# Mean squares moved to ScalarE, and the values of two batches made beside the first GLU, in a two-layer gated cross-attention kernel

## Chip, cores and metric

The kernel runs on one core of a Trainium2 chip. The metric is the device time of one execution in microseconds (us), as the median of several runs. Before the change it is 2046.36 us, the median of three runs from 2041.12 to 2047.37. Five engines work side by side: TensorE (PE, matrix products), VectorE (DVE), ScalarE (ACT), GpSimd (POOL) and SyncE (SP), which here issues the DMA transfers. PEld is the weight load of PE.

## The reference, cut to what matters

The input x has 4 batches of 512 rows with 512 columns. Four gated residual parts follow one another: a state space scan, a GLU with quantised weights (the "bitnet"), a cross-attention with 16 heads of 128, and four small experts. The attention is the part that the change touches:

```
q = (hidden_states @ Wq).reshape(B, Sq, H, D)
k = (encoder_hidden_states @ Wk).reshape(B, Skv, H, D)
v = (encoder_hidden_states @ Wv).reshape(B, Skv, H, D)
q = rmsnorm(q, gq)
k = rmsnorm(k, gk)
scores = jnp.einsum('bqhd,bkhd->bhqk', q, k) * scale
attn = jax.nn.softmax(scores, axis=-1)
out = jnp.einsum('bhqk,bkhd->bqhd', attn, v)
```

Here rmsnorm is x * rsqrt(mean(x * x) + eps) * g. The values v depend on the context and on Wv alone, not on x, so they can be made at any time once both are there.

## The kernel before

**Numbers in halves.** Almost every 32-bit matrix operand is held as two 16-bit pieces, a high part hi and a remainder lo, and one product is three matmuls (mm3, L241). The helper split (L236) makes the two pieces: ScalarE writes hi (L238), then VectorE computes w * S - hi into lo (L239). Nearly all matmuls share L247, so the text tells them apart by the name of the result: pw is a piece of the values, pk of the keys, pq of the queries, ps of the scores, pav of the weighted sum.

**The stages.** A prologue runs the scan of batch 0 and then its GLU (bitnet(0), L1190). Beside it the kernel makes the values of batch 0 (first_values, L1198), stages the weights of the first four heads (L1200) and makes their keys (L1201). The prologue's tiles lie in the pool pro (L1142). When that pool is given back, a pool named at (L1204) takes the room, and it holds nearly all the tiles of the attention. The main loop (L1228) then walks over 4 x 16 heads. Under the attention of batches 0, 1 and 2 it lays the scan and the GLU of the next batch; under that of batch 3 it lays the experts of the first three batches. The experts of the last batch end the program.

**Values.** For a group of four heads hg, values_of (L348) makes four pieces of 128 rows, each by six matmuls into one PSUM bank and a split. For batches below PRE (here 1) first_values (L358) does this in the prologue. It loads Wv, takes its norm (L365), splits it (L366) and stores it to DRAM; then each piece is written to a tile ov, of which there are VB = 2, and stored to DRAM (L374). In the attention, values(hg) (L830) loads these pieces back with four DMAs (L838) into tiles named v, of which there are AV = 4. For the other batches values(hg) loads the split Wv (L842) and calls values_of in the attention itself, with the same tiles.

**Keys and query norms.** keys (L779) makes one piece of 128 rows by six matmuls. ScalarE sums the squares of each of four heads (L802). A VectorE instruction turns the sums into mean + eps, ssk (L805); GpSimd takes the power -1/2, rk (L178, called at L807); VectorE multiplies (L813); ScalarE and GpSimd split the result (L820, L822); two transposing DMAs store it as kT (L824). query_norms (L862) sums the squares of the queries on PE (psq, L868), VectorE adds eps and scales, ssq (L873), GpSimd takes the power, rqs (L178, called at L875), and ScalarE uses rqs in nmx (L896) and in the exponential pr (L904).

**What sets the order.** Every engine works its own queue in order. The queues are laid out at build time: the program's order is the rank, and a simulated timeline (L1342) fills an engine's free time with later work that is ready in it. So the pieces of the values, which come in the program after the GLU, can run inside it. All DMAs go through the one queue of SP, and a DMA at its head that waits holds up those behind it.

Of the kernel before, what the change touches and what calls it, by code (L numbers as in the profile page):

```python
# [29 lines left out]
F32 = mybir.dt.float32  # L30
# [4 lines left out]
AF = mybir.ActivationFunctionType  # L35
ALU = mybir.AluOpType
# [4 lines left out]
P = 128  # L41
B = 4
L = 512
T = 4
# [7 lines left out]
HD = 128  # L52
# [7 lines left out]
QS = 2.0**-11  # L60
KS = 1024.0
# [38 lines left out]
VB = 2  # L100
# [2 lines left out]
ABUF = {"m": 2, "s": 2}  # L103
LO_POOL = {(b, h, 1) for b in range(3) for h in range(9, 16)}
HL = 2
PRE = 1
LEADS = {1: 12, 2: 16, 3: 16}
LEAD_B = 6

# [2 lines left out]
def flamingo_kernel(  # L112
# [8 lines left out]
    nc = tc.nc  # L121
# [114 lines left out]
    def split(w, hi, lo, S):  # L236

        nc.scalar.activation(hi, w, AF.Copy, scale=S)  # L238
        nc.vector.scalar_tensor_tensor(lo, w, S, hi, ALU.mult, ALU.subtract)  # L239

    def mm3(ps, pairs, first=True, last=True):  # L241

        n = 3 * len(pairs)
        i = 0
        for lh, ll, rh, rl in pairs:
            for l, r in ((lh, rh), (lh, rl), (ll, rh)):
                nc.tensor.matmul(ps, l, r, start=first and i == 0, stop=last and i == n - 1)  # L247
                i += 1
# [3 lines left out]
    Sq, Sk, Sv, So, ceq = [], [], [], [], []  # L252
# [9 lines left out]
    def run(steps):  # L262
        while True:
            try:
                next(steps)
            except StopIteration as e:
                return e.value
# [60 lines left out]
    def attention_weights(hg, ps_pool, staging):  # L328
        cols = slice(hg * 512, (hg + 1) * 512)
        d, S, _ = yield from staging(f"wq{hg}", Wq[hg], HG, ps_pool)  # L330
        wq_d.append(d)
        Sq.append(S)
        d, S, _ = yield from staging(f"wk{hg}", Wk[:, cols].rearrange("(k p) c -> p k c", p=P), 1, ps_pool)
        wk_d.append(d)
        Sk.append(S)
        d, S, _ = yield from staging(f"wo{hg}", Wo[cols, :].rearrange("(h p) f -> p h f", p=P), HG, ps_pool)
        wo_d.append(d)
        So.append(S)

        c = const.tile([P, 1], F32, name=f"ceq{hg}")  # L340
        nc.vector.tensor_scalar(c, Sq[hg][:, 1:2], XS * QS * (HD * EPS) ** 0.5, None, ALU.mult)
        nc.vector.tensor_tensor(c, c, c, ALU.mult)
        ceq.append(c)

    wv_d = []
    v_d = [[dram.tile([P, T, 1024], F16, name=f"vd{b}{hg}") for hg in range(NG)] for b in range(PRE)]

    def values_of(b, hg, wv, ps_tile, v_tile):  # L348

        for c in range(T):  # L350
            rows = slice(c * P, (c + 1) * P)
            ps = ps_tile(f"pw{b}{hg}{c}")
            mm3(ps, [(cT[b][:, 0, k, rows], cT[b][:, 1, k, rows], wv[:, 0, k], wv[:, 1, k]) for k in range(2)])
            v = v_tile([P, 2, 512], F16, f"v{b}{hg}{c}")
            split(ps, v[:, 0], v[:, 1], QS)
            yield v

    def first_values(pool, ps_tile):  # L358


        for hg in range(NG):
            raw = pool.tile([P, 2, 512], F32, tag="rv", name=f"rawv{hg}", bufs=2)
            nc.sync.dma_start(raw, Wv[:, hg * 512 : (hg + 1) * 512].rearrange("(k p) c -> p k c", p=P))
            wv = pool.tile([P, 2, 2, 512], F16, tag="wv", name=f"wv{hg}", bufs=2)
            S = frobenius(raw, wv[:, 0], psv, f"wv{hg}")  # L365
            split(raw, wv[:, 0], wv[:, 1], S[:, 1:2])  # L366
            Sv.append(S)
            wv_d.append(dram.tile([P, 2048], F16, name=f"dwv{hg}"))
            nc.sync.dma_start(wv_d[hg], wv.rearrange("p s k c -> p (s k c)"))
            for b in range(PRE):  # L370
                for c, v in enumerate(
                    values_of(b, hg, wv, ps_tile, lambda s, d, n: pool.tile(s, d, tag="v", name=f"o{n}", bufs=VB))
                ):
                    nc.sync.dma_start(v_d[b][hg][:, c, :], v.rearrange("p s c -> p (s c)"))  # L374
                    yield
# [109 lines left out]
    gfac = const.tile([P, 1], F32, name="gfac")  # L485
# [276 lines left out]
    def attention(b):  # L762
# [16 lines left out]
        def keys(hg, ps_tile=ap):  # L779

            nm = f"{b}{hg}"
            wk = ak.tile([P, 2, 2, 512], F16, tag="wk", name=f"wk{nm}", bufs=1)
            nc.sync.dma_start(wk.rearrange("p s k c -> p (s k c)"), wk_d[hg])

            sck = sm(1, "sck", f"sck{nm}")
            nc.vector.tensor_scalar(
                sck, Sc[b][:, 1:2], Sk[hg][:, 1:2], EPS**0.5 / KS, ALU.mult, ALU.mult
            )
            nc.vector.tensor_tensor(sck, sck, sck, ALU.mult)
            kTs = []  # L790
            for pair in range(2):
                kTs.append(ak.tile([P, T, 2, 2, P], F16, tag="kT", name=f"kT{nm}{pair}", bufs=KT))
            kns[hg] = kTs
            for c in range(T):
                rows = slice(c * P, (c + 1) * P)
                ps = ps_tile(f"pk{nm}{c}")
                mm3(ps, [(c_[:, 0, k, rows], c_[:, 1, k, rows], wk[:, 0, k], wk[:, 1, k]) for k in range(2)])
                sq = ak.tile([P, L], F32, tag="sq", name=f"ksq{nm}{c}", bufs=2)
                ssk = sm(HG, "ssk", f"ssk{nm}{c}")
                for h in range(HG):  # L800
                    cols = slice(h * HD, (h + 1) * HD)
                    nc.scalar.activation(  # L802
                        sq[:, cols], ps[:, cols], AF.Square, accum_out=ssk[:, h : h + 1]
                    )
                nc.vector.tensor_scalar(ssk, ssk, 1.0 / (HD * KS * KS), sck, ALU.mult, ALU.add)  # L805
                rk = sm(HG, "rk", f"rk{nm}{c}")
                rsqrt(rk, ssk)  # L807
                if b in KACT:
                    for h in range(HG):
                        cols = slice(h * HD, (h + 1) * HD)  # L810
                        nc.scalar.activation(sq[:, cols], ps[:, cols], AF.Copy, scale=rk[:, h : h + 1])
                else:
                    nc.vector.tensor_tensor(  # L813
                        sq.rearrange("p (h d) -> p h d", h=HG), ps.rearrange("p (h d) -> p h d", h=HG),
                        rk.unsqueeze(2).to_broadcast([P, HG, HD]), ALU.mult,
                    )

                ks = ak.tile([P, 2, 2, 2 * HD], F16, tag="ks", name=f"ks{nm}{c}", bufs=2)
                kn = sq.rearrange("p (a d) -> p a d", a=2)
                (nc.vector.tensor_copy if KSD else nc.scalar.copy)(ks[:, :, 0], kn)  # L820
                eng = nc.vector if (b, hg) in KLD else nc.gpsimd
                eng.tensor_tensor(ks[:, :, 1], kn, ks[:, :, 0], ALU.subtract)  # L822
                for pair in range(2):
                    nc.sync.dma_start_transpose(  # L824
                        kTs[pair][:, c].rearrange("p s h r -> p (s h) r"),
                        ks[:, pair].rearrange("p s d -> p (s d)"),
                    )
                yield

        def values(hg):  # L830
            def v_tile(shape, dtype, name):
                return at.tile(shape, dtype, tag="v", name=name, bufs=AV)

            if b < PRE:
                vals[hg] = []
# [26 lines left out]
        def query_norms(i):  # L862
            hg, h = divmod(i, HG)
            hn = f"{b}{hg}{h}"
            sq = kqs[i][2]
            ps = ap(f"psq{hn}")
            for c in range(T):
                nc.tensor.matmul(  # L868
                    ps[:, c : c + 1], sq[:, c * P : (c + 1) * P], ones[:, 0:1],
                    start=True, stop=True,  # L870
                )
            ssq = sm(T, "ssq", f"ssq{hn}")
            nc.vector.tensor_scalar(ssq, ps[:, 0:T], ceq[hg], gfac, ALU.add, ALU.mult)  # L873
            rqs = sm(T, "rqs", f"rqs{hn}")
            rsqrt(rqs, ssq)  # L875
            kqs[i][2] = rqs
# [88 lines left out]
        def step(i, phase):  # L965
# [4 lines left out]
            if phase == 0:  # L970
                if h == 0:
# [3 lines left out]
                    if KL == 0 and kns[hg] is None:  # L975
                        run(keys(hg))
                    if b < PRE:
                        values(hg)
# [163 lines left out]
    with tc.tile_pool(name="pro", bufs=1) as pro, tc.tile_pool(name="psp", bufs=4, space=PSUM) as psp:  # L1142
# [52 lines left out]
        def aside(name):  # L1195
            return psum(pss, name)

        run(first_values(pro, aside))  # L1198
        for hg in range(EARLY):
            stage_attention_weights(hg, pss)  # L1200
        run(keys(0, aside))  # L1201
    psa = ctx.enter_context(tc.tile_pool(name="psa", bufs=4, space=PSUM))
    at_pool = ctx.enter_context(ExitStack())
    at = at_pool.enter_context(tc.tile_pool(name="at", bufs=1))  # L1204
# [22 lines left out]
    n = B * NH  # L1227
    for i in range(-2, n):  # L1228
# [13 lines left out]
        s = steps[(i + 1) // NH]((i + 1) % NH, 1) if 0 <= i + 1 < n else iter(())  # L1242
        w = steps[i // NH](i % NH, 2) if i >= 0 else iter(())
        for k, g in enumerate((q, s, q, s, w, s, w, s, w, q)):
# [7 lines left out]
            if k in KPOS:  # L1252
                j, c = divmod((i + 2) * len(KPOS) + KPOS.index(k) - KOFF, 4 * len(KPOS))
# [92 lines left out]
```

## Time and profile before

| what | value |
|---|---|
| median of three runs | 2046.36 us |
| the profiled execution | 2033.87 us |
| its span, first to last instruction | 2032.1 us |
| mean granted clock of PE | 0.882 |
| busy: PE, DVE, ACT, POOL | 1588.9, 1596.6, 1269.7, 1003.6 us |
| share of the span: PE, DVE, ACT, POOL | 78%, 79%, 62%, 49% |
| DMA queue of SP: bytes, share of 16 engines' span | 356.36 MB, 69.1% |

No engine is the limit from end to end, so the shares are read by stretch. The view of busy time by stretch gives, for each piece of the span, how long each engine worked in it; an engine that works nearly all of a piece is what that piece waits for. The groups of instructions by name give counts, durations and waits. The timeline lists instructions in order, with the idle time before each and what ended it.

### The profile page before, as it was taken

How to read it: one execution, taken by the hardware profiler on the slowest of the kernel's cores; microseconds unless marked ns; L12 is line 12 of the kernel's file. 1: busy time of each engine (PE TensorE's matmuls, PEld its weight loads, DVE VectorE, ACT ScalarE, POOL GpSimd, SP SyncE). 2: the span in 40 equal slices, each digit the busy share in tenths (PEclk: the TensorE clock that was granted, in tenths of full speed). 3: DMA queues.
4: the chain of work that ended last, by engine and by line, in shares of the span. 5: the costliest groups of instructions: out<-in, count | busy, mean ns of one | idle time of the engine just before them, and what ended most of it. 6: DMA issues, size and time to landing. Idle time of an engine off the chain costs nothing. (4 is left out here: it accounts for less than half of the span.)

```text
span 2032.1 us, 26952 instructions
## 1 busy us (share of the span) xinstructions
PE 1588.9 (78%) x8238; PEld 896.8 (44%) x8238; DVE 1596.6 (79%) x2975; ACT 1269.7 (62%) x2962; POOL 1003.6 (49%) x920
## 2 busy tenths in 40 slices
PE   4465855886768968788698977788989879798888
PEld 2343322444444424455444434455444445445446
DVE  6798984789999866999898669999985565655654
ACT  6786565766557565665447674656565676757653
POOL 1984341367676454867545367775354440413211
PEclk8555977888789979898799988899999999998999
DMA  7454468678889764777867568688675877857754
GB/s 258 155 194 157 126 172 248 154 204 179 209 239 221 169 126 133 182 180 185 204 144 160 113 156 222 163 194 225 164 158 125 175 171 198 193 171 171 193 123 136
DMA packets 525201, 358.07 MB, mean 176 GB/s; under 512 B 424768, under 2 KB 427456, under 8 KB 519040
## 3 DMA queue, kind: packets, MB, share of 16 engines
q1 hardware_dynamic: 525056, 356.36, 69.1%
q8 instruction: 64, 1.05, 0.2%
q14 instruction: 81, 0.66, 0.1%
HBM read 214.98 MB, written 38.54 MB: 125 GB/s over the span
## 5 line engine op out<-in xcount | busy, mean ns | idle before, releaser
L181 POOL TENSOR_TENSOR h<-du,bc 128x512 f32<-128x512 f32 x256 | 332.8, 1320 | 74.5 <-PE py L578 57.6
L578 PE MATMUL py<-ident,h 128*128 128x128 f32 x1024 | 194.1, 337 | 91.3 <-DVE h L603 74.3
L595 ACT ACTIVATE dA<-delta,A 128x512 f32<-128x512 f32 x256 | 171.7, 684 | 144.7 <-DVE h L603 113.1
L247 PE MATMUL ps<-kT,qT 128*128 128x512 f16 x768 | 212.8, 397 | 54.4 <-ACT pr L904 43.0
L602 DVE TENSOR_TENSOR_SCAN dA<-dA,h 128x512 f32<-128x512 f32 x200 | 240.6, 1218 | 10.3 <-ACT dA L595 7.0
L247 PE MATMUL pq<-axnT,wq 128*128 128x512 f16 x768 | 213.7, 437 | 41.4 <-DMA axnT<-xsa 15.5
L247 PE MATMUL pav<-pT,v 128*128 128x256 f16 x1536 | 200.2, 283 | 42.5 <-DVE v L239 14.5
L578 PEld LDWEIGHTS py<-ident,h 128*128 128x128 f32 x1024 | 164.7, 214 | 130.8 <-DVE h L603 100.6
L925 DVE SCALAR_TENSOR_TENSOR hl<-pr,den,hl 128x512 f16<-128x512 f32 x214 | 194.6, 924 | 26.5 <-ACT hl L922 15.0
L904 ACT ACTIVATE pr<-ps,nmx,rqs 128x512 f32<-128x512 f32 x256 | 197.7, 775 | 24.3 <-DVE hl L925 20.3
L884 DVE TENSOR_REDUCE nmx<-ps 128x1 f32<-128x512 f32 x256 | 172.8, 681 | 46.9 <-PE ps L247 46.3
L247 PEld LDWEIGHTS <-v 128*128 128x128 f16 x1536 | 154.2, 102 | 96.1 <-issue 33.7
L247 PE MATMUL pwo<-wo,oT 128*128 128x512 f16 x768 | 183.0, 389 | 11.6 <-DVE oT L239 4.5
L247 PEld LDWEIGHTS <-wq 128*128 128x128 f16 x768 | 84.3, 111 | 160.3 <-issue 96.8
L924 POOL TENSOR_SCALAR hl<-pr,den 128x512 f16<-128x512 f32 x86 | 63.3, 736 | 183.9 <-DVE den L911 107.3
L247 PEld LDWEIGHTS <-cT 128*128 128x128 f16 x768 | 79.7, 104 | 148.2 <-issue 78.2
L247 PEld LDWEIGHTS <-qT 128*128 128x128 f16 x768 | 77.7, 102 | 139.8 <-issue 76.1
L896 ACT ACTIVATE nmx<-nmx,rqs 128x1 f32<-128x1 f32 x256 | 69.3, 293 | 107.6 <-POOL rqs L178 64.7
L603 DVE TENSOR_TENSOR h<-dA,cc 128x512 f32<-128x512 f32 x200 | 134.0, 679 | 2.7
L181 POOL TENSOR_TENSOR g<-g,gv 128x512 f32<-128x512 f32 x64 | 84.2, 1318 | 95.2 <-DVE gv L707 44.8
L247 PE MATMUL pk<-wk,cT 128*128 128x512 f16 x384 | 107.9, 424 | 27.2 <-DVE ssq L873 15.9
L178 POOL TENSOR_TENSOR rqs<-ssq,mhalf 128x4 f32<-128x4 f32 x64 | 68.6, 1072 | 121.6 <-DVE ssq L873 112.0
(381 smaller groups left out, 3505.7 us busy)
## 6 DMA issues: line engine op xcount, KB each, us to landing
bc<-bd SPq DMA_DIRECT2D x112, 256.0 KB, 4.2
cc<-bd SPq DMA_DIRECT2D x112, 256.0 KB, 4.3
wq<-dwq SPq DMA_DIRECT2D x64, 256.0 KB, 3.9
wo<-dwo SPq DMA_DIRECT2D x64, 256.0 KB, 4.2
w<-w3d SPq DMA_DIRECT2D x12, 1024.0 KB, 7.1
g<-in_gate_b SPq DMA_DIRECT2D x48, 256.0 KB, 3.9
gv<-in_val_b SPq DMA_DIRECT2D x48, 256.0 KB, 4.1
de<-hle SPq DMA_DIRECT2D x9, 1024.0 KB, 4.8
```

What stands on the lines that cost most here:

```text
L178: nc.gpsimd.tensor_tensor(res, arg, mhalf[:, : arg.shape[1]], ALU.pow)
L181: nc.gpsimd.tensor_tensor(out, a, b, ALU.mult)
L247: nc.tensor.matmul(ps, l, r, start=first and i == 0, stop=last and i == n - 1)
L578: nc.tensor.matmul(ys[g // gs][:, g % gs, t, :], src[:, g::T], ident, is_transpose=True, start=first and t == 0 and g % gs == 0, stop=last ...
L595: last = nc.scalar.activation(dA, delta[:, t0 + t, :], AF.Exp, scale=A[:, t0 + t, n : n + 1])
L602: nc.vector.tensor_tensor_scan(dA, dA, h, 0.0, ALU.mult, ALU.add)
L603: nc.vector.tensor_tensor(h, dA, cc, ALU.mult)
L884: nc.vector.tensor_reduce(nmx[:, c : c + 1], ps, AX.X, ALU.max, negate=True)
L896: nc.scalar.activation(nmx[:, one], nmx[:, one], AF.Copy, scale=rqs[:, one])
L904: mark[0] = nc.scalar.activation(pr, scs[c], AF.Exp, bias=nmx[:, one], scale=rqs[:, one], accum_out=den[:, c - c0 : c - c0 + 1],).ins
L924: nc.gpsimd.tensor_scalar(hl[:, c, 0], prs[c], den[:, one], 1.0, ALU.mult, ALU.mult)
L925: nc.vector.scalar_tensor_tensor(hl[:, c, 1], prs[c], den[:, one], hl[:, c, 0], ALU.mult, ALU.subtract)
```

## The change

It has three parts.

1. The two small instructions ssk and ssq go from VectorE to ScalarE. ScalarE computes scale * in + bias, so ssq's form (p + c) * g becomes p * g + c * g, and ceq is multiplied by gfac once for each group of heads.
2. PRE becomes 2: the values of batch 1 are also made in the prologue, stored, and loaded back. In the prologue a new helper splits a piece without VectorE: ScalarE writes the scaled piece as 32 bit into a new tile vf (one buffer), then hi from it, and GpSimd subtracts.
3. first_values is called after the staging of the first weights and after the first keys, not ahead of them.

```diff
-PRE = 1
+PRE = 2
...
+    def split_aside(w, hi, lo, S, v):
+
+        nc.scalar.activation(v, w, AF.Copy, scale=S)
+        nc.scalar.copy(hi, v)
+        nc.gpsimd.tensor_tensor(lo, v, hi, ALU.subtract)
...
         nc.vector.tensor_tensor(c, c, c, ALU.mult)
+        nc.vector.tensor_tensor(c, c, gfac, ALU.mult)
         ceq.append(c)
...
-    def values_of(b, hg, wv, ps_tile, v_tile):
+    def values_of(b, hg, wv, ps_tile, v_tile, aside=None):
...
-            split(ps, v[:, 0], v[:, 1], QS)
+            if aside is None:
+                split(ps, v[:, 0], v[:, 1], QS)
+            else:
+                split_aside(ps, v[:, 0], v[:, 1], QS, aside([P, 512], F32, f"vf{b}{hg}{c}"))
...
-                    values_of(b, hg, wv, ps_tile, lambda s, d, n: pool.tile(s, d, tag="v", name=f"o{n}", bufs=VB))
+                    values_of(
+                        b, hg, wv, ps_tile, lambda s, d, n: pool.tile(s, d, tag="v", name=f"o{n}", bufs=VB),
+                        lambda s, d, n: pool.tile(s, d, tag="vf", name=n, bufs=1),
+                    )
...
-                nc.vector.tensor_scalar(ssk, ssk, 1.0 / (HD * KS * KS), sck, ALU.mult, ALU.add)
+                nc.scalar.activation(ssk, ssk, AF.Identity, bias=sck, scale=1.0 / (HD * KS * KS))
...
-            nc.vector.tensor_scalar(ssq, ps[:, 0:T], ceq[hg], gfac, ALU.add, ALU.mult)
+            nc.scalar.activation(ssq, ps[:, 0:T], AF.Identity, bias=ceq[hg], scale=gfac)
...
-        run(first_values(pro, aside))
+
         for hg in range(EARLY):
             stage_attention_weights(hg, pss)
         run(keys(0, aside))
+        run(first_values(pro, aside))
```

## Prediction

> **What bounds the kernel now.** I read the page's slices of the span first, then the busy time of each engine in stretches of 20 and 25 us, then the groups behind the instructions that the change touches, and the timeline around the first GLU. In the slices each digit is the busy share of about 51 us, in tenths:
>
> ```profile
> PE   4465855886768968788698977788989879798888
> DVE  6798984789999866999898669999985565655654
> ACT  6786565766557565665447674656565676757653
> POOL 1984341367676454867545367775354440413211
> ```
>
> DVE stands at 9 through the scans under batches 0, 1 and 2 and at 8 beside the first GLU (slices 5 and 6). PE leads between the scans and from slice 31 on. ACT is never full. So work taken from DVE pays in about half of the span, work taken from PE in the other half, and ACT has room. In the stretches of 20 us of the prologue's end, the columns after the times are PE, PEld, DVE, ACT and POOL busy:
>
> ```profile
> 200.00:220.00 20.00, 18.81 (x87) 8.58 (x86) 17.97 (x42) 10.14 (x17) 6.81 (x6) 0.97 0.54 162
> ...
> 240.00:260.00 20.00, 16.89 (x79) 7.66 (x78) 19.06 (x43) 9.88 (x17) 6.21 (x6) 1.00 0.43 126
> 260.00:280.00 20.00, 9.38 (x31) 3.54 (x29) 18.87 (x46) 12.68 (x24) 7.53 (x8) 0.82 0.69 196
> ...
> 300.00:320.00 20.00, 5.12 (x16) 1.87 (x16) 10.98 (x26) 7.48 (x18) 8.20 (x8) 0.67 0.76 196
> ```
>
> Up to 280 us DVE binds (19 of 20), ACT is half and POOL a third busy; then nothing is full. What ends the prologue is the last row tile of the GLU, whose transposed result the first queries need:
>
> ```profile
> 303.90 5.12 PE L732 MATMUL po<-w,hqT 128*128 128x512 fp8e4 x16 [7.28 <-DMA hqT<-hq]
> 322.68 5.09 PE L247 MATMUL pq<-axnT,wq 128*128 128x512 f16 x12 [13.65 <-DMA axnT<-xsa]
> ```
>
> **Part 1, ssk and ssq.** What leaves DVE:
>
> ```profile
> L805 DVE TENSOR_SCALAR ssk<-ssk,sck x64: 199/228/3332, 292.5 to 1869.5; 128x4 f32<-128x4 f32 x64
> L873 DVE TENSOR_SCALAR ssq<-psq,ceq,gfac x64: 250/275/283, 332.6 to 1957.5; 128x4 f32<-128x4 f32 x64
> ```
>
> The triplet is least, median and greatest ns. ssq costs 64 x 0.27 = 17.5 us. ssk should cost 64 x 0.21 = 13 us, but sums to about 28.6 us, because some take up to 3.33 us, in scans where POOL is over 70% busy. Only what lies in stretches that DVE fills counts. Of the 25 us stretches, 22 have DVE at 23.2 or more; they hold 12.8 us of ssk and 4.8 us of ssq, 17.5 together. The gain is between nothing (the freed time goes to the next DVE instruction that is held the same way, or to a scan that still waits for its dA) and 17.5; I take 12, two thirds: DVE is at 97% there, but the scan also waits for ACT at times.
>
> ACT gets 128 instructions. Rows for a short ACT instruction are den (L910) with no pointer operand, 0.205 us, and nmx (L896) with one, 0.293. A second pointer: xna (L202, two) takes 0.811 against 0.592 for sq (L859, none), so two cost 0.22. Hence ssk 0.29 and ssq 0.205 + 0.22 = 0.42, together 64 x 0.71 = 45 us; the ends are 0.205 and 0.42 each, 26 to 54 us. This lies in ACT's free 38% and costs nothing where DVE or PE binds; were ACT full, it would cost all 45. The four products for ceq are 0.15 us each on DVE, once. What may cost is the wait: ssq stands in ACT's queue until PE has ended psq, with the next exponentials dA and pr behind it. DVE sat 14.8 us, in 11 cases, in just this wait. ACT's wait can cost nothing up to 14.8; I take 3, since ACT's own sq feeds psq and so stands close by, and a scan's DVE chain has other work meanwhile. Chains get a hop shorter too (sums and ssk are now both ACT's): POOL idled 63.2 us behind ssk and 112.0 behind ssq, but POOL binds nowhere, so nothing. Part 1: **-9**, from -17.5 to +15.
>
> **Part 2 in batch 1.** The values leave the attention. By stretch (PE, DVE, ACT busy on them), with the heads of the four groups:
>
> ```profile
> 800.00:825.00 25.00, 5.82 (x24) 2.05 (x3) 2.33 (x4) 0.96 0.82 239
> ...
> 925.00:950.00 25.00, 5.67 (x24) 2.69 (x4) 2.34 (x4) 0.97 0.79 190
> ...
> 1050.00:1075.00 25.00, 3.62 (x16) 2.73 (x4) 1.78 (x3) 1.00 0.80 164
> ...
> 1125.00:1150.00 25.00, 4.21 (x18) 0.87 (x2) 1.18 (x2) 1.00 0.45 106
> ```
>
> The first two groups lie where DVE binds: 2.7 + 2.7 = 5.4 us of DVE. The last two lie where PE does (24.0 of 25 from 1025, 24.9 from 1125): 2 x 5.8 = 11.5 us of PE. At most 17; I take 5 + 8 = 13, since the PE stretches have holes (20.3 and 22.5 in the neighbours). In place come 16 loads of 256 KB for four of 512 KB. They stand in SP's queue, ahead of the transposed probabilities, and the four tiles v come free only with the last weighted sum of the group before. Nothing to 4 x 4.9 us (the landing time of these loads in batch 0); I take 3, near nothing, since in batch 0 no idle time before pav is put down to them. Part 2 here: **-10**, from -17 to +3.
>
> **Parts 2 and 3 in the prologue.** DVE loses 16 pieces x 0.68 = 10.9 us of the 81 that it works from 195 to 283. Keys and weights rank ahead of the values now, so their splits leave the GLU's end, where DVE is not full. ACT gets 32 x (0.60 + 0.62) = 39 us (rows ov and the cast ks, L820) for 9.5: from 195 to 320 it goes from 66 busy to 95. POOL gets 32 x 1.16 = 37 us (row ks, L822) on 45, so 82 of 125. PE gets 16 x 6 matmuls, 23 us by the 23 that batch 1's took. All fit, side by side.
>
> Whether the pieces also fit one after the other is the question, since vf is single: the next piece cannot begin before GpSimd is done with this one. The period is at least 0.60 + 0.62 + 1.16 = 2.4 us. The old pieces came at (258 - 198) / 16 = 3.75 us each among the same neighbours. So 32 pieces take 77 to 120 us. If they begin at 198 as now, they end between 275 and 318: inside the time that the prologue has, up to 322.7. What the wait for GpSimd holds up: in ACT's queue the Tanh of the GLU behind vf; in SP's queue the transposes hqT and axnT behind 32 stores instead of 16 (the old ones held SP 18 us for 16, 0.32 each had they not waited); in POOL's queue the product g of the GLU.
>
> A second cost is shown by one place in the timeline:
>
> ```profile
> 247.56 4.16 DVE L728 TENSOR_SCALAR hq<-g 128x512 bf16<-128x512 f32 x4
> ```
>
> These four take 0.42 each elsewhere; here POOL works without a break, from 247.1 to 251.1, and they take 1.04. Twelve hq to 283 us lost 2.6 us with POOL busy a third; with it two thirds busy I put 3 us more on DVE. The Trainium skill, "SBUF — State Buffer", on the two sides of the memory, says that VectorE in a two-port mode and GpSimd exclude each other for a whole instruction. It fits this row and ssk's 3.33 us, and speaks for part 1 and against part 2: were all 24 such instructions of the GLU caught at half of 1.16 us, they would lose 14 us, and the sum of this part would be +6 in place of -5.
>
> I take -11 + 3 + 3 (for the queues): **-5**, from -11 to +20 (worked out below).
>
> **Sum.** -9 - 10 - 5 = -24 us. The profiled execution took 2033.87 us (span 2032.1 and 1.8 around it), so 2010. It was 12.5 us under the median of the runs, 2046.36; the difference carries over to the median: **2022 us**.
>
> **Rivals.** Each is told as a time of the median.
>
> *More than that.* If DVE's relief counts in full and the GLU's end gets free of keys and weights, the ends add up to -17.5 - 17 - 11 = -46: 2000. For it: the DVE digits. Against it: PE, at 7 or 8 in the same slices, is next.
>
> *Moved, not saved.* The work was only changed for other work: the freed DVE time is lost again to waits of ACT for psq and to GpSimd's new work, and the tail of the values falls among the first heads. Then part 1 gives -3, batch 1 -7 and the prologue +8, in all -2: 2044. ACT's room (62%) speaks against it, the one queue of each engine for it.
>
> *Slower: the values come late.* Ranked behind weights and keys, they fill holes only. If they take their turn when the keys do (pk ran at 286 to 294), and not at 198, they end at 290 + 77 = 367 to 410. The room of pro is what at is laid in, and the first loads into it (v at 314.4) follow the last matmul on pro's weights (309.0). If the attention then waits for vf and the stores, its first queries move from 322.7 to 367 or later: +44 here, less 19 for the other parts, +25 at the least: 2071. It decides once the values end 24 us past 322.7, at 347. Against it: the old ones too were ranked behind the whole GLU and ran inside it, and ACT is idle half of 200 to 280.
>
> *It does not do what it says.* That the values do not run beside the GLU is this last rival; the move of ssk and ssq cannot fail to happen.
>
> **How the numbers follow.** Forecast 0.48 (-24, between -38 and -8: 2008 to 2038), more 0.18 (2000), moved 0.13 (2044), slower 0.21 (2071). A measurement tells about 0.3% from no change, 6 us. Faster: 0.48 + 0.18 and a fifth of moved, 0.68; within: 0.10; slower: 0.21 and a little of moved, 0.22. The range leaves out part of more below 1996 and part of slower above 2066.
>
> **What would show it.** Right: ssk and ssq of about 0.3 and 0.4 us on ACT; DVE some 55 us less busy in all (28.6 + 17.5 + 10.9 for each of two batches makes 68, less what is held elsewhere); the pieces of the values 2.4 to 3.75 us apart, from about 198 and done by 320; the first pq at or ahead of 322; batch 1 some 10 us shorter. Wrong: pieces first at 280, or the first pq later than 330; idle time of ACT before ssq beyond 15 us; pav waiting for v in batch 1; hq and the other fast DVE instructions mostly at 1 us.

## The result, and the profile after

After the change the median is **2057.64 us** (eight runs, 2051.70 to 2067.87), against 2042.88 us for eight runs of the kernel before (2035.53 to 2047.37). The ratio is 1.0068, with a 95% interval from 1.0049 to 1.0087: by the ratio slower by some 14 us (the two medians lie 14.8 apart), where 24 us less was forecast. The profiled executions have spans of 2049.9 and 2032.1 us.

The page of the kernel after, section 2, has the same slices, now of 51.2 us:

```profile
PE   4463784777677788778789887877989879798988
DVE  6798772779998886999989779999985565554654
ACT  6786665875745567666656775656566686767653
POOL 1984564267675544776745547767453440313211
```

DVE still stands at 8 and 9 through the same three blocks. Beside the first GLU (slices 5 and 6) it fell from 9 and 8 to 7 and 7, as meant. The slice to look at is the seventh (307.5 to 358.7 us): DVE fell there from 4 to 2 and PE from 5 to 4, where the attention should begin. The next view of the kernel after, busy time in stretches of 20 us (PE, PEld, DVE, ACT, POOL, then clock and DMA), shows the hole itself:

```profile
240.00:260.00 20.00, 19.33 (x84) 8.26 (x83) 15.48 (x40) 13.21 (x22) 9.90 (x9) 0.93 0.59 138
260.00:280.00 20.00, 17.55 (x84) 8.15 (x83) 18.46 (x37) 12.90 (x22) 14.78 (x14) 1.00 0.60 171
...
300.00:320.00 20.00, 15.02 (x64) 6.26 (x63) 5.25 (x14) 12.56 (x21) 10.26 (x11) 0.93 0.54 157
320.00:340.00 20.00, 13.83 (x50) 5.52 (x49) 0.63 (x5) 8.50 (x14) 8.71 (x8) 0.88 0.31 119
340.00:360.00 20.00, 0.59 (x2) 0.50 (x2) 7.11 (x23) 10.26 (x21) 5.85 (x7) 0.55 0.73 254
```

From 320 to 340 us nothing is full: PE makes pieces of the values, and DVE works 0.63 us. From 340 to 360 PE works 0.59 us; before, it worked 15.73 there. The timeline of PE in the kernel after says what stands on either side of the hole:

```profile
304.61 3.62 PE L745 MATMUL po<-w,hqT 128*128 128x512 fp8e4 x16
...
366.10 4.26 PE L253 MATMUL pq<-axnT,wq 128*128 128x512 f16 x12 [0.94 <-DMA wq<-dwq]
```

The GLU's last row tile stands where it stood (303.90 before), and the DMA that transposes its result starts at 316.38. But the first queries wait until 366.10: 43.4 us later than before. What lies between is in the queue of SP (start, length, line, transfer):

```profile
321.13 22.25 SPq L387 DMA_DIRECT2D vd<-ov  x9
...
348.25 2.88 SPq L387 DMA_DIRECT2D vd<-ov  x2
...
358.13 1.74 SPq L851 DMA_DIRECT2D v<-vd  x4
359.91 0.91 SPq L862 DMA_DIRECT2D wq<-dwq  x2
```

The values' stores run until 351. Only then come the loads of the attention's own tiles: the first v at 358.13 (314.43 before), then the weights for the first queries. The view of what the queue of SP waited for in these microseconds (line, what ended the wait, us in all, times, longest) names the store:

```profile
SPq L796 <- DMA dwk<-hlwk: 4.6, 1, 4.6
SPq L851 <- DMA vd<-ov: 1.3, 1, 1.3
```

The first line is the load of a weight, wk, that stands ahead of v in the queue; the second is v itself. The last store of a piece is issued at 350.82 and lands at 357.98, and the first load of v starts 0.14 us later. The last pieces of the values hold the attention back.

Why they are so late is in two more views. The group of vf gives count, least, median and greatest ns, first and last start; the timeline of ACT shows the rhythm:

```profile
L243 ACT ACTIVATE vf<-pw x32: 570/597/598, 245.6 to 348.3; 128x512 f32<-128x512 f32 x32
```

```profile
335.37 0.60 ACT L243 ACTIVATE vf<-pw 128x512 f32<-128x512 f32 x1 [1.32 <-POOL ov L245]
336.00 0.62 ACT L244 CAST ov<-vf 128x512 f16<-128x512 f32 x1
337.94 0.60 ACT L243 ACTIVATE vf<-pw 128x512 f32<-128x512 f32 x1 [1.32 <-POOL ov L245]
338.57 0.62 ACT L244 CAST ov<-vf 128x512 f16<-128x512 f32 x1
```

The pieces begin at 245.6, not at 198: Wv's split now stands behind the weights and keys, and the first of its four parts begins at 238.4 (192.1 before). In the clear stretch one piece follows the other every 2.57 us, with ACT idle for 1.32 of it until GpSimd is done with the only vf. Over all 32 the mean is (350.8 - 245.6) / 32 = 3.3 us.

Batch 1 is relieved as the diff says. The stretches of the kernel after, for the pieces of the values alone (PE, DVE, ACT), are empty where before they took 5.82 us of PE:

```profile
800.00:825.00 25.00, 0.00 (x0) 0.00 (x0) 0.00 (x0) 1.00 0.92 208
```

The delay can be followed through the whole program. The first product of each scan that is laid under an attention, pin, is a good milestone. Timelines of PE, the first and the third of these scans, before:

```profile
365.38 5.34 PE L247 MATMUL pin<-cT,inp 128*128 128x512 f16 x24
...
1155.53 1.03 PE L247 MATMUL pin<-cT,inp 128*128 128x512 f16 x4
```

and after:

```profile
385.03 4.69 PE L253 MATMUL pin<-cT,inp 128*128 128x512 f16 x21
...
1174.46 3.83 PE L253 MATMUL pin<-cT,inp 128*128 128x512 f16 x17
```

The three scans begin 20, 21 and 19 us late, and the end comes 17.8 us late: the delay that is there by 385 us stays with the scans. The heads do not simply carry it along. Those of batch 1 catch up: their last weighted sum ends 18 us earlier than before (1211.7 against 1230.0), and the sums of batch 2 begin 16 us earlier (1250.3 against 1266.6). But beside the third scan the sums of batch 2 take 374 us from first to last, where they took 341, and those of batch 3 begin 15 us late (1646.0 against 1630.6). So what batch 1 gained is lost again under batch 2. That the late scan is what holds the heads there is read from these times and not tested.

### The profile page after: what moved, and what is told of

The parts are those of the page before. It is cut to its first block, busy times and chain, and to the rows that moved or that the text cites. A ratio compares the mean times of both kernels' runs of the same rounds, so it can differ in the third digit from the quotient of the medians.

```text
span 2049.9 us, 27132 instructions
## 1 busy us (share of the span) xinstructions
PE 1590.2 (78%) x8238; PEld 899.7 (44%) x8238; DVE 1577.1 (77%) x2819; ACT 1321.6 (64%) x3124; POOL 1038.9 (51%) x952
## 5 line engine op out<-in xcount | busy, mean ns | idle before, releaser
L253 PE MATMUL pav<-pT,v 128*128 128x256 f16 x1536 | 208.2, 290 | 57.2 <-DMA pT<-hl 22.8
L938 DVE SCALAR_TENSOR_TENSOR hl<-pr,den,hl 128x512 f16<-128x512 f32 x214 | 204.5, 970 | 31.5 <-ACT hl L935 18.0
L253 PEld LDWEIGHTS <-v 128*128 128x128 f16 x1536 | 158.3, 104 | 113.7 <-issue 54.3
L253 PEld LDWEIGHTS <-oT 128*128 128x128 f16 x768 | 75.4, 99 | 98.3 <-issue 7.6
```

Of the source, the lines that this page charges most:

```text
L938: nc.vector.scalar_tensor_tensor(hl[:, c, 1], prs[c], den[:, one], hl[:, c, 0], ALU.mult, ALU.subtract)
```

## The experiments

Theory **L**: the values end late, the attention waits for them, and this costs more than batch 1 gives. Rivals: **W**, the cost is ACT's wait for psq in front of ssq (part 1); **O**, the keys' and values' new order; **P**, the 16 loads in batch 1 and the work beside the GLU. In the course of it came **N**: the queues are laid out anew at build time for every edit, and the new layout moves the time by itself.

All ratios are to the kernel before. First pq is the start of the first queries, and the last columns are the starts of the three scans under an attention, in us.

| kernel | ratio, 95% interval | first pq | scans begin |
|---|---|---|---|
| before | 1 | 323 | 365, 749, 1156 |
| after | 1.0068, 1.0049 to 1.0087 | 366 | 385, 770, 1174 |
| part 1 alone | 0.9988, 0.9965 to 1.0010 | 325 | 364, 749, 1154 |
| all but part 1 | 1.0144, 1.0127 to 1.0162 | 362 | 385, 775, 1171 |
| values ahead of the keys | 1.0098, 1.0076 to 1.0119 | 345 | 399, 784, 1168 |
| after, PRE = 1 | 0.9964, 0.9944 to 0.9984 | 334 | 353, 729, 1143 |
| two vf | 1.0096, 1.0072 to 1.0120 | 366 | 389, 781, 1165 |
| two vf, three ov | 0.9993, 0.9975 to 1.0012 | 340 | 383, 759, 1141 |
| split by DVE again | 0.9986, 0.9966 to 1.0006 | 350 | 393, 762, 1141 |
| split by DVE, PRE = 1 | 1.0060, 1.0035 to 1.0085 | 332 | 346, 741, 1161 |
| before + pebble, place 0 | 0.9979, 0.9950 to 1.0007 | 323 | 366, 756, 1153 |
| before + pebble, place 4 | 1.0029, 1.0010 to 1.0048 | 325 | 367, 756, 1154 |
| after + pebble | 1.0047, 1.0022 to 1.0073 | 362 | 382, 772, 1164 |
| PRE = 1 + pebble | 0.9984, 0.9966 to 1.0002 | 333 | 353, 740, 1144 |
| late end, no gain | 1.0186, 1.0138 to 1.0234 | 386 | 379, 779, 1191 |
| gain, no late end | 0.9828, 0.9796 to 0.9859 | 333 | 352, 732, 1121 |
| two vf, groups 0 and 1 only | 0.9927, 0.9898 to 0.9956 | 330 | 371, 749, 1137 |
| two vf, PRE = 1 | 0.9969, 0.9948 to 0.9990 | 325 | 344, 736, 1139 |
| two vf, groups 2 and 3 only | 1.0030, 1.0009 to 1.0051 | 334 | 378, 768, 1161 |
| groups 0 and 1 + pebble | 1.0010, 0.9993 to 1.0027 | 331 | 372, 755, 1148 |

**Part 1 alone, on the kernel before.**

```diff
-                nc.vector.tensor_scalar(ssk, ssk, 1.0 / (HD * KS * KS), sck, ALU.mult, ALU.add)
+                nc.scalar.activation(ssk, ssk, AF.Identity, bias=sck, scale=1.0 / (HD * KS * KS))
...
-            nc.vector.tensor_scalar(ssq, ps[:, 0:T], ceq[hg], gfac, ALU.add, ALU.mult)
+            nc.scalar.activation(ssq, ps[:, 0:T], AF.Identity, bias=ceq[hg], scale=gfac)
```

> The kernel before with part 1 alone: ssk and ssq on ScalarE. Theory L (the loss is the late end of the prologue: the values start at 246 instead of 198 us, go one after the other every 2.57 us, and the attention's tiles wait for the last of them): the prologue ends as before, first pq at 322 +- 5, and the time is below before by some 5 to 12 us, ratio 0.994 to 0.998. Rival W (the loss is ScalarE's wait for psq, 60.6 us in 20 cases after the change where VectorE had 14.8 in 11): ratio 1.003 to 1.01, with idle time of ScalarE before ssq of 40 us or more.

Measured 0.9988: nothing that can be told from no change, though ACT waits 48.7 us for psq in it. Such a wait by itself does not make the loss.

**All but part 1.** The two lines of after go back to VectorE.

```diff
-                nc.scalar.activation(ssk, ssk, AF.Identity, bias=sck, scale=1.0 / (HD * KS * KS))
+                nc.vector.tensor_scalar(ssk, ssk, 1.0 / (HD * KS * KS), sck, ALU.mult, ALU.add)
...
-            nc.scalar.activation(ssq, ps[:, 0:T], AF.Identity, bias=ceq[hg], scale=gfac)
+            nc.vector.tensor_scalar(ssq, ps[:, 0:T], ceq[hg], gfac, ALU.add, ALU.mult)
```

> The changed kernel with part 1 undone: ssk and ssq on VectorE again, parts 2 and 3 kept. Theory L: the first pq stays at 360 to 370 us and the time is still above before, ratio 1.006 to 1.014. Rival W: the time falls back to before or below, ratio 0.995 to 1.002, though the first pq is as late.

Measured 1.0144, with the first pq at 362. W would have this faster than after; it is slower by 0.0076, so with the run above W falls.

**The order undone.** The values are called ahead of the keys again.

```diff
+        run(first_values(pro, aside))
         for hg in range(EARLY):
...
-        run(first_values(pro, aside))
```

> The changed kernel with part 3 undone: the first values are called ahead of weights and keys again, with two batches and the split on ScalarE and GpSimd. Theory L: the values start near 198 us, take 32 x 2.6 to 3.3 us and end at 281 to 305; the first pq comes at 320 to 335, and the time is 10 to 25 us below the changed kernel, ratio to before 0.990 to 1.001. Rival W, and a rival P (the loads of the second batch's values and the added work of GpSimd cost the time, whatever their place): ratio 1.004 to 1.010 as after the change.

Measured 1.0098, outside L's range and inside that of its rivals. The pieces now run from 199 to 326, 4.0 us each, so they end later than L had it (281 to 305) and near the latest end that the prediction reckoned with (318). The keys, which then stand behind 32 pieces, come at 337, the first queries at 345, and the scan begins at 399. So with two batches the old order is no better. That clears the new order only for this kernel; the pair for one batch follows below.

**PRE = 1 in the kernel after.**

```diff
-PRE = 2
+PRE = 1
```

> The changed kernel with values of batch 0 only in the prologue (PRE = 1); order, split and part 1 kept. Theory L: 16 values from 246 on, every 2.6 to 3.6 us, end at 290 to 303, beside the GLU's end, so the first pq is at 318 to 330; the work of batch 1's values is back in the attention; ratio to before 0.995 to 1.003. Rival W: ratio 1.004 to 1.010. Rival P: as theory L, so this run alone does not tell P from L; the place of the first pq does (P: it does not matter for the end).

Measured 0.9964, as L had it, though the chain of 16 pieces ends at 321, later than the 290 to 303 expected, and the first queries come later too. The timeline of PE in this kernel:

```profile
334.20 4.60 PE L253 MATMUL pq<-axnT,wq 128*128 128x512 f16 x12 [6.05 <-DMA wq<-dwq]
...
353.24 4.69 PE L253 MATMUL pin<-cT,inp 128*128 128x512 f16 x21
```

The first queries come 32 us earlier than in the kernel after, 13 us behind the last piece (15 there), and the scan as much earlier. The loss goes with the second batch of part 2.

**A second vf** (room for it was made by giving up the second raw tile of Wv), then **a third ov** as well.

```diff
-            raw = pool.tile([P, 2, 512], F32, tag="rv", name=f"rawv{hg}", bufs=2)
+            raw = pool.tile([P, 2, 512], F32, tag="rv", name=f"rawv{hg}", bufs=1)
...
-                        lambda s, d, n: pool.tile(s, d, tag="vf", name=n, bufs=1),
+                        lambda s, d, n: pool.tile(s, d, tag="vf", name=n, bufs=2),
```

> The changed kernel with two buffers for vf (and one in place of two for the raw Wv, for room). Theory L (single vf makes a chain of 2.57 us a piece; it ends at 351 and holds the attention): in the stretch after the GLU, where the pieces stood 2.57 us apart, they come every 1.3 to 1.9 us; the last is done at 310 to 330, the first pq comes at 325 to 345, and the time falls by half or more of what PRE = 1 gave: ratio to before 0.994 to 1.002. Rival P (two batches in the prologue cost the time for their loads and work, not for the late end): ratio 1.004 to 1.010.

Measured 1.0096: L's expectation failed here, and the ratio lies in P's range. The single vf is not what the end hangs on: the pieces end at 348.0, 3 us earlier. The timeline of ACT shows the next wait in line, the store of the two ov tiles:

```profile
333.32 0.62 ACT L244 CAST ov<-vf 128x512 f16<-128x512 f32 x1 [1.06 <-DMA vd<-ov]
333.85 0.59 ACT L243 ACTIVATE vf<-pw 128x512 f32<-128x512 f32 x1
335.26 0.60 ACT L243 ACTIVATE vf<-pw 128x512 f32<-128x512 f32 x1 [0.82 <-POOL ov L245]
335.84 0.62 ACT L244 CAST ov<-vf 128x512 f16<-128x512 f32 x1
337.45 0.62 ACT L244 CAST ov<-vf 128x512 f16<-128x512 f32 x1 [0.99 <-DMA vd<-ov]
```

Two pieces take 4.1 us. With three ov tiles as well (VB = 3):

> As the run with two vf, and three output tiles ov in place of two. If the stores to DRAM (two tiles ov, 2.3 us to land) then set the rhythm, the pieces come up to 0.5 us closer and the first pq 5 to 15 us earlier than with two vf alone; if ScalarE or GpSimd does, within 3 us. Ratio to before 0.992 to 1.002 by theory L, 1.004 to 1.010 by rival P.

the pieces end at 329, the first pq stands at 340, 26 us earlier than with two vf alone, and the ratio is 0.9993, 0.75% under after. This is in L's range and not in P's: all the work and all the loads of two batches are in this kernel, and only the end is earlier. Too few tiles are what made the chain long: two of ov as much as one of vf.

**The old split by DVE**, with PRE = 2 and with PRE = 1.

```diff
-                        lambda s, d, n: pool.tile(s, d, tag="vf", name=n, bufs=1),
```

> The changed kernel with the old split (ScalarE and VectorE) for the first values, no vf; two batches, behind the keys, part 1 kept. Theory L: VectorE has 32 x 0.68 = 22 us more in the prologue, but no chain through vf; the pieces start at 240 to 250 and come every 1.6 to 3 us, last at 300 to 330, first pq at 325 to 345; ratio 0.996 to 1.004. Rival P: 1.004 to 1.010.

> The kernel before with part 1 and the new order alone: values of batch 0 only, old split, behind the keys. It tells what the new split is worth beside one batch of values, against the run with PRE = 1 (0.9964). If the split by GpSimd frees VectorE as was forecast: ratio 0.998 to 1.003, some 5 to 10 us above that run. If the order alone makes the gain: the same as that run, 0.994 to 0.998, with the scan of batch 1 (first pin) at 353 us again.

Measured 0.9986 and 1.0060. The first has the ratio that L forecast, though its pieces end at 339 and its first pq stands at 350, both later than L had them. The second fits neither forecast: its pieces end at 305 and its first scan begins at 346, earlier than in any kernel of two batches, and yet it is slower than before. From the second scan to the third it takes 420 us, where the kernel before takes 406. No theory had that, and it gave rise to N. This kernel is also the test of O with one batch: it differs from part 1 alone (0.9988) in the order only, and it is 0.72% slower, with intervals that do not meet. So the new order can cost time by itself, and O is not excluded; one layout of each was run.

**Pebbles.** Four copies of one column to a tile that nobody reads, at one of two places of the main loop.

```diff
+        if i == 0:
+            with tc.issue_after(mark[0]):
+                for _ in range(4): nc.scalar.copy(sm(1, "nul", f"nul{i}{_}"), tg[:, 0:1])
```

> The kernel before with a pebble: four ScalarE copies of 128x1 (about 0.2 us each, 0.8 us in all, result unused) queued behind one exponential at the first head (i = 0). It changes no work that anybody waits for, but the order of each queue behind it is planned anew. Theory L (times follow the late end of the prologue and the work moved): ratio 0.998 to 1.002. Rival R (any edit that moves the plan shifts the time by up to 1%, so a share of the change's 0.7% belongs to no part of it): off by more than 0.3% in this run or in another of the four, either way.

> The same pebble in the kernel before, at the fifth head (i = 4). Theory L: ratio 0.998 to 1.002. Rival R: as for the other pebbles; the time from the first scan's start to the end differs from before by up to 20 us, with no common direction.

> The changed kernel with the pebble at the first head. The prologue (first query product at 366 us) is as in the changed kernel. Theory L: ratio to before 1.005 to 1.009. Rival R: anywhere from 0.998 to 1.016.

> The changed kernel with PRE = 1 (measured at 0.9964) and the pebble at the first head. Theory L: ratio 0.994 to 0.999 again. Rival R: anywhere from 0.990 to 1.007; above 1.000 would mean that the gain of that run was of the plan, not of the edit.

The pebble moves the kernel before by -0.21% and +0.29%, after by -0.21%, PRE = 1 by +0.20%. The intervals reach 0.2 to 0.3% to either side, so part of this is the scatter of the runs; the second pebble is clear of it (1.0010 to 1.0048). So differences under some 0.3% say nothing here of the edit, and the loss of after (0.68 and 0.47%) is above that, but not far. One more pebble, further down, moved a kernel by 0.83%, more than the whole loss.

**The late end by itself.** PRE = 1, and 16 more pieces that go through vf, ov and a store to a place that nobody reads: the chain of after without its gain.

```diff
+  nc.scalar.activation(vf, raw[:, 0], AF.Copy, scale=QS)
+  nc.scalar.copy(nv[:, 0], vf)
+  nc.gpsimd.tensor_tensor(nv[:, 1], vf, nv[:, 0], ALU.subtract)
+  nc.sync.dma_start(nul_d[hg][:, c, :], nv.rearrange("p s c -> p (s c)"))
```

> The changed kernel with PRE = 1, and 16 dummy pieces in the place of batch 1's: the same copies, subtraction and store through the same single vf, from the raw weights, no matmuls, results unused. The chain of 32 pieces is as long, nothing is taken from batch 1's attention. Theory L: first query product at 355 to 370, ratio 1.006 to 1.020, that is 0.8 to 2% above PRE = 1 without them (0.9964, with a pebble 0.9984). Rival P (the loads of batch 1's values in the attention cost the time): ratio 0.996 to 1.002.

**The gain by itself.** PRE = 2, but the prologue makes the values of batch 0 alone and batch 1 loads those.

```diff
-    v_d = [[dram.tile([P, T, 1024], F16, name=f"vd{b}{hg}") for hg in range(NG)] for b in range(PRE)]
+    v_d = [[dram.tile([P, T, 1024], F16, name=f"vd{b}{hg}") for hg in range(NG)] for b in range(1)]
+    v_d.append(v_d[0])
...
-            for b in range(PRE):
+            for b in range(1):
```

> The changed kernel without the making of batch 1's values: its attention loads batch 0's stored ones instead, so batch 1's result is left wrong; all loads, waits and tiles of the attention are as after the change. It shows what the moved work gives when it costs nothing. Theory L: first query product at 325 to 340 as with PRE = 1; the time from the first scan's start to the third's falls by 10 to 30 us; ratio 0.983 to 0.994. Rival P: ratio 0.998 to 1.006, no better than PRE = 1.

The pair is the plainest result, since its differences are larger than that of any pebble. Against PRE = 1 (0.9964) the late end costs 2.22% or 45 us; the last piece of batch 0 is done at 364.6 and the last dummy at 370.2, and the first queries come at

```profile
385.97 2.75 PE L253 MATMUL pq<-axnT,wq 128*128 128x512 f16 x12
```

in place of 334.20: 52 us later, 0.87 us of time for each. (The 45 us hold the copies and subtractions of the dummies too; the run with three ov has the same work, with an earlier end, and stands at 0.9993.) The gain is 1.36% or 28 us, nearly three times the 10 that were forecast, in the one layout that was run. The kernel with the gain alone and the kernel after differ in one thing, the making of batch 1's values in the prologue: it costs 2.40% or 49 us, with first queries 33 us later. In the kernel with the gain alone the stretch that was empty after is full:

```profile
332.94 4.72 PE L253 MATMUL pq<-axnT,wq 128*128 128x512 f16 x12 [5.30 <-DMA wq<-dwq]
```

```profile
340.00:360.00 20.00, 17.51 (x95) 9.35 (x95) 14.35 (x34) 17.59 (x44) 4.60 (x6) 1.00 0.70 205
```

The 16 loads are in this kernel too, so P falls as far as the loads go.

**Half of it.** With the longer buffers, only two of the four groups of batch 1 are made in the prologue; and, beside them, PRE = 1 with these buffers.

```diff
-            for b in range(PRE):
+            for b in range(PRE if hg < 2 else 1):
...
-            if b < PRE:
+            if b < 1 or b < PRE and hg < 2:
```

> The changed kernel with two vf, three ov, one raw Wv, and the values of batch 1 made early for the first two of the four groups only (24 pieces for 32). Theory L: last piece at 300 to 320, first query product at 328 to 345, half of the gain in batch 1: ratio 0.990 to 0.998. Rival P: 0.998 to 1.006. By the pebbles 0.3% either way says nothing.

> The changed kernel with PRE = 1, two vf, three ov, one raw Wv. Theory L: the 16 pieces end at 290 to 305 instead of 320, the first query product comes at 322 to 332 instead of 334, ratio 0.992 to 0.999. If the single vf does not matter with one batch: 0.996 to 1.000, like PRE = 1.

> As the version with half of batch 1's values (0.9927), but for groups 2 and 3 instead of 0 and 1; the prologue is the same, first query product at 325 to 340. If the gain comes from relief of VectorE beside the scan: ratio 0.997 to 1.001, no better than PRE = 1. If PE's relief in the later groups pays as well, as the prediction had it (8 of 13 us): 0.990 to 0.995.

> The version with the values of groups 0 and 1 (0.9927) with the pebble of four ScalarE copies at the first head. If its gain is its own: ratio 0.989 to 0.997. If it was of the plan: 0.997 to 1.001.

PRE = 1 with these buffers gave 0.9969, like PRE = 1 without them, though its first queries come 10 us earlier. Groups 0 and 1 gave 0.9927, the best time of the study among kernels that do the whole work, and groups 2 and 3 gave 1.0030, which fits neither forecast for it. But groups 0 and 1 with a pebble gave 1.0010. So 0.8% hangs on the layout of the queues here, and neither the better half nor a better kernel is shown.

## Why the prediction was wrong, step by step

**The step that failed** is "If they begin at 198 as now, they end between 275 and 318: inside the time that the prologue has, up to 322.7." They began at 246, because Wv's load and split rank behind weights and keys too, and ended at 351. The period was inside the range given (3.3 us of 2.4 to 3.75); the start was not reckoned with, though part 3 of the diff is what moves it. The sum thus took the prologue's part as -5 us, and gave the late end a chance of 0.21 as a rival; measured by the pair of kernels that differ in it alone, making batch 1's values there costs 49 us. The rival "the values come late" had the mechanism: it set the point of decision at 347, and the values end at 351. That its first queries, at 367, came out right (366.10) is partly luck: it let the pieces begin at 290 and come every 2.4 us, where they began at 246, came every 3.3 and were followed by 15 us until the first queries. It forecast 25 us more than before, and some 14 were measured.

**The delay's price.** The rival took the 44 us in full. A late end alone cost 0.87 us for each us of the first pq; that is the ratio of one pair, in which the first scan moved by 26 us and the second by 50, and no rule. By it, the 32 us between PRE = 1 and after cost 28, the gain gives 28 back, and after should stand where PRE = 1 does. It stands 1.04% above, and with pebbles on both 0.63% above: 13 to 21 us are **not settled**. The layout of the queues can be part of it (0.2 to 0.8% by the pebbles). Another part may be that the gain is smaller when batch 1 begins late: from first to last weighted sum its heads take 390 us with PRE = 1, 361 with the gain alone and 373 in the kernel after. Why these 12 us are missing was not tried apart.

From before to after, one edit at a time, the runs give -0.12% for part 1, +0.72% for the new order, -0.96% for the new split and +1.04% for the second batch. Each of these is one pair, and a pebble moved one kernel by 0.83%, so how the loss divides among the edits is not shown.

Over more layouts there is a mean. The seven kernels that make and use the values of both batches begin the first scan 31 us later than the eight with PRE = 1, the kernel before among these (388 and 357), and the third 10 us later (1160.5 and 1150.4): two thirds of the delay are won back, most of it between the second scan and the third, though in the kernel after itself nothing was. Their mean ratios are 1.0062 and 0.9997, 0.65% apart. But these kernels differ in more than PRE. The pairs that differ in PRE alone give +1.04, +0.63 (with pebbles) and +0.24% (longer buffers) for the second batch, and with the split by DVE -0.74%. A loss of about this size fits, and is not shown to be more than layout.

**What makes the attention wait** can be read in the traces. In twelve kernels, after among them, the first load of v starts 0.06 to 0.15 us after the last store of the prologue's pieces has landed; in the kernel before it comes 52 us after. The first pq follows the last piece by 10 to 19 us in every kernel with a late chain. In the kernel with the late end alone that store is one of the dummies, which v never reads, and the view of what SP waited for names it in front of v:

```profile
SPq L859 <- DMA nd<-nv: 2.5, 1, 2.5
```

So the wait is not for the data of the values. That it is the room of pro, in which tiles of at lie and which comes free only with pro's last user, fits this and was not tested: a place of their own for these tiles was not tried.

**Part 1, -9 forecast.** Alone it gave -0.12% (2.4 us, from 7 less to 2 more). On top of the other parts it gave -0.76%, of which the layout may be a part. Of the two instructions, ssk cost what was forecast and ssq less:

```profile
L818 ACT ACTIVATE ssk<-ssk,sck x64: 281/302/337, 217.7 to 1888.7; 128x4 f32<-128x4 f32 x64
L886 ACT ACTIVATE ssq<-psq,ceq,gfac x64: 335/354/403, 373.7 to 1975.1; 128x4 f32<-128x4 f32 x64
...
  PE psq L881: 60.6, 20
```

0.30 and 0.35 us, for 0.29 and 0.42. (The Trainium skill, "ScalarE: Activation LUTs", in its section on what ACT_TABLE_LOAD costs, gives 186 ns plus about 93 ns for each pointer operand and 0.833 ns for each element. By that page an estimate for four elements is 0.28 us with one pointer and 0.375 with two; the trace agrees within about 0.02.) The wait was mis-sized: the view of what ACT waited for before ssq, the last line above, has 60.6 us in 20 waits, four times the bound of 14.8 that DVE's waits had given. The wait of one engine was no bound for that of another in the same place. It cost nothing that the runs show.

**DVE 55 us less busy.** It was 19.5 (1596.6 to 1577.1). Removed were 68; the instructions' own times fell by 41 only, because others grew, hl (L938) by 9.9 us and hq by 4.4 most, and the rest is overlap that the busy time counts once. The four new products for ceq took 2.5 us, where 0.15 each was forecast. The prediction counted on less DVE time where DVE binds, and part of what was removed came back as longer times of its neighbours.

**Fast instructions of DVE beside POOL, +3.** In the first GLU, which the term was for, the 16 hq went from 11.0 to 12.4 us, half of what was taken; in all four batches hq went from 37.0 to 41.4, its median from 422 to 427 ns. (The prediction's estimate by the rule of the Trainium skill, "SBUF — State Buffer", on the two separate sides, with every such instruction caught, was 14 us for the first GLU alone. Single instructions take up to 1.49 us after and 1.48 before, which fits the rule, but the typical one is not held. Nor does the rule as the prediction put it, held for one whole instruction, reach the 3.33 us of ssk: in the trace of before three GpSimd instructions of 1.26 us run beside that one, back to back.)

**Batch 1, -10.** The gain by itself is 28 us. The term had taken only the freed time of the engine that is full in each stretch, DVE 5 and PE 8. Its reading of the third group's stretch was incomplete: before, DVE (the third busy time of the row) works all of it, while PE, named as the limit, works 24.03.

```profile
1025.00:1050.00 25.00, 24.03 (x115) 11.23 (x114) 25.00 (x57) 9.90 (x21) 9.21 (x8) 1.00 0.60 151
```

Two smaller readings are off as well: DVE stands at 9 and 8 in slices 5 and 6, not at 8 in both, and 25 stretches, not 22, have DVE at 23.2 or more; the sums over them are right. The loads, taken at +3, are never named in front of a weighted sum. What the other 15 us of the gain are was not taken apart.

**The prologue, -5.** DVE is freed beside the GLU, but that frees no time there: the GLU's last row tile ends at 308.2, against 309.0 before. Less work on the engine that is fullest brought the end of this stage nearer by less than 1 us, where 11 had been counted.

## What to carry to other kernels

When work is moved out of a full stretch into "free" time, work out three dates for the chain: when its first input is there in the new order, how long one round of its tiles takes with the buffers that it has, and what waits for its end, the next user of its memory among them. Here the capacity of the engines said nothing about these. Price the gain and the delay apart, each with a kernel that has only the one: here they were 28 and, for 52 us of delay, 45 us, and their difference is of the size of one change of layout. Where a build lays out the queues anew, run the kernel with a harmless extra instruction first; a difference below what that makes is not a result of the edit.

## What the runs showed that was not expected

Four idle instructions on ScalarE moved the time by 0.2 to 0.3% in three kernels and by 0.8% in a fourth. A second tile for vf alone moved the end of the chain by 3 us, since the store of ov, at 4.1 us for two pieces, stood right behind it: three ov tiles were needed as well for 21 us.
